# A depthwise convolution's third input tile, prepared one layer earlier: where the transposes, the residual store and the first weights are placed

## The chip, the cores and the metric

The kernel runs on one core of one Trainium2 chip. The metric is the device time of one execution in microseconds. The core has a matrix engine (PE), a vector engine (DVE), a scalar engine (ACT), a general engine (POOL) and a queue engine (SP) that here only issues transfers. Sixteen DMA engines move data between DRAM and the on-chip memory; transfers are issued by SP, by ACT (most weight loads) and by POOL.

## The reference

Input `x` has 8 images of 384 channels of 32x32, all in fp32. Four layers follow, each `x = x + f(groupnorm(x))` with 32 groups:

- layer 0: three depthwise 3x3 convolutions, attention over the 1024 positions with 8 heads, a projection
- layer 1: four experts, each 384 -> 384 -> 384 with ReLU; the two best per position are weighted
- layer 2: a depthwise 7x7 convolution with reflected edges, plus a bias:

```
xp = jnp.pad(x, ((0, 0), (0, 0), (3, 3), (3, 3)), mode='reflect')
out = lax.conv_general_dilated(xp, w, (1, 1), 'VALID', feature_group_count=C) + b
```

- layer 3: three branches of small MLPs and depthwise convolutions (1, 3 and 5), a softmax fusion of them and a projection

The change lies in what layer 1 hands to layer 2, and in layer 2.

## The kernel before

The 384 channels are NC = 3 tiles (`ct`) of P = 128 partitions; B = 8 images of N = 1024 positions. In the profiled execution layer 0 lasts to about 1770 us, layer 1 runs from about 1819 to 2896, layer 2 from 2911 to 3113 and layer 3 from 3123 to the end.

**Layer 1** goes image by image, each in two halves `h` of HF = 512 positions. `experts` loops over 12 pairs of expert and hidden tile. For each, `hidden` does three matmuls (L763) and a ReLU on ACT (L767); DVE multiplies the hidden tile by the expert's coefficient row (L961); three matmuls (L976) add it into three accumulators. The coefficient row `cb` is loaded by `coefs` (L942) from DRAM (`cfmem`) and spread over the partitions, one for each expert and half, from a pool of 5 buffers; the same row times the second bias is added into the residual `r` on DVE (L966). At the end of a half DVE adds the accumulators into `r` (L982). `residual` (L740 to L745) loads and builds the next image's `r`, partly on DVE (L745). In this layer the tile scheduler fixes the order of instructions on each engine from the program; each engine then runs its own order, waiting on semaphores.

When an image is done, `pass_on(r, b)` runs. It stores the finished residual to `r2mem`, for later addition (L1004): for each tile four transfers of 32 partitions, with the channels permuted. It takes the image's group statistics, and for each tile it writes the normalized image `xn2` (affine, ACT L204). Layer 2 wants the image transposed in blocks of 32x32, with three reflected rows at each end (HP = 38 rows instead of H = 32). For tiles 0 and 1 `transpose_in` does that at once into `xts[0]` and `xts[1]`, which stay on the chip: a DVE transpose (L989) and two POOL copies of the edges (L992, L993). For tile 2 there is no third such tile yet: `xn2` is stored as it is to `x2mem` (L1017).

**Layer 2** is written as banded matmuls (L1327): for each tile 16 weight tiles (8 values of `c`, two halves `e`) with 28 matmuls of 256 columns each. A weight tile is made in two steps. `load_weights` loads two of them at once as `w` (L1052, issued by ACT; the first two by SP), and POOL adds the edge columns (L1056). `next_weights` spreads one into `wx` with two ACT instructions (L1068), from a pool of three that opens when layer 1's pools close, and it calls `load_weights` after each second one. From layer 2 on the order of instructions is the written one.

During tile 1 of layer 2, `prepare(b)` (L1163) makes `xts[2]`, in the memory of `xts[0]`, two images after each of four steps: load from `x2mem` (L1168), then `transpose_in`. The output of a tile is evicted by ACT (L1268) and finished during the next tile by `finish` (L1174 to L1206): DVE transposes it back (L1180), SP loads the stored residual (`r2`, L1183), DVE adds it with the bias (L1185), SP stores the sum (`y2mem`, L1188), and DVE takes statistics. `finish_all` runs these steps for the eight images at a pace given by a table of counts, one count for each `c`.

**Transfers.** Each issuing engine handles its transfers in the order written, and waits in front of one until what it needs is there. SP's and ACT's transfers also share eight completion counters, given out in program order: a transfer that gets a counter first waits until the transfer that had it before, most often the one eight places earlier, has landed. If that one was issued by the other engine, the two queues are tied together.

Of the kernel before, what the change touches and what calls it, by code (L numbers as in the profile page):

```python
# [11 lines left out]
FP = mybir.dt.float32  # L12
# [6 lines left out]
P = 128  # L19
B, C, H, W = 8, 384, 32, 32  # L20
N = H * W
NC = C // P
HF = 512
# [32 lines left out]
K7, R7 = 7, 3  # L56
HP = H + 2 * R7
# [13 lines left out]
def img(a):  # L71
    return a.rearrange("p (h w) -> p h w", w=W)
# [3 lines left out]
def conv_mixer_kernel(ctx: ExitStack, tc: tile.TileContext, a: dict, out: bass.AP):  # L76
    nc = tc.nc
# [5 lines left out]
    dram = ctx.enter_context(tc.tile_pool(name="raw", bufs=1, space=DRAM))  # L83
# [42 lines left out]
    with tc.tile_pool(name="gprep", bufs=1) as gp, tc.tile_pool(  # L126
        name="gpsum", bufs=2, space=PSUM
# [115 lines left out]
    with (  # L243
# [9 lines left out]
        with tc.tile_pool(name="cx", bufs=4) as cx, tc.tile_pool(  # L253
            name="cgn", bufs=2, space=PSUM
        ) as cgn:
            for b in range(B):
                x = cx.tile([P, NC - 1, N], FP, tag="x", name="x")
# [457 lines left out]
    pre_pool.close()  # L715


    r2mem = [dram.tile([P, B, N], FP, tag=f"r2_{ct}", name=f"r2_{ct}") for ct in range(NC)]
    x2mem = dram.tile([P, B, N], FP, tag="x2m", name="x2mem")
    y2mem = [dram.tile([NC, P, N], FP, tag=f"y2_{b}", name=f"y2_{b}") for b in range(B)]  # L720
    mv3 = const.tile([P, 2, NC, B], FP, name="mv3")

# [215 lines left out]
    ex = ewpool.enter_context(tc.tile_pool(name="ex", bufs=2, reuse_waits="tile"))  # L938

    def coefs(b, h, e):  # L940
        cb = ex.tile([P, HF], FP, tag="cb", name="cb", bufs=5)
        nc.sync.dma_start(  # L942
            out=cb,
            in_=cfrows[2 * b + h : 2 * b + h + 1, e * HF : (e + 1) * HF].to_broadcast([P, HF]),
        )
        return cb
# [37 lines left out]

    xts = []

    def transpose_in(xt, b, xn):

        nc.vector.transpose(  # L989
            xt[:, :, b, R7 : R7 + H].rearrange("p c h -> p h c"), img(xn)  # L990
        )
        nc.gpsimd.tensor_copy(xt[:, :, b, 0:R7], xt[:, :, b, 2 * R7 : R7 : -1])  # L992
        nc.gpsimd.tensor_copy(  # L993
            xt[:, :, b, R7 + H : HP], xt[:, :, b, R7 + H - 2 : H - 2 : -1]
        )

    def new_xt(pool):
        return pool.tile([P, 32, B, HP], FP, tag="xt", name="xt")

    def pass_on(r, b):  # L1000

        for ct in range(NC):
            for i in range(4):
                nc.sync.dma_start(  # L1004
                    out=r2mem[ct][:, b, :].rearrange("(d b a r) n -> a b d r n", a=2, b=2, d=2)[
                        i // 2, i % 2
                    ],
                    in_=r[32 * i : 32 * i + 32, ct, :],
                )
        s, t = gn_coefs(image_stats(r), eh, "sm")  # L1010
        for ct in range(NC):
            xn2 = ex.tile([P, N], FP, tag="xn2", name="xn2")
            affine(xn2, r[:, ct, :], s[:, ct : ct + 1], t[:, ct : ct + 1])
            if ct < 2:
                transpose_in(xts[ct], b, xn2)
            else:
                nc.sync.dma_start(out=x2mem[:, b, :], in_=xn2)  # L1017

    for b, h in EARLY:
        experts(rs[b].tile, b, h)  # L1020
# [12 lines left out]
    lw = lwpool.enter_context(  # L1033
        tc.tile_pool(name="lw", bufs=2, side="right", reuse_waits="tile")
    )
    parity = lw.tile([P, 2], FP, name="parity", bufs=1)
    nc.gpsimd.memset(parity, 0.0)
    for i in range(4):
        nc.gpsimd.memset(parity[32 * i : 32 * i + 32, i % 2 : i % 2 + 1], 1.0)
    WPARTS = {K7: 2, 5: 2, 3: 1}  # L1040
    weights, loaded = {}, []
    todo_load = [(K7, ct, c) for ct in range(NC) for c in range(8)]
# [18 lines left out]
    def next_weights():  # L1061
        if not loaded:
            return
        key, w = loaded.pop(0)
        n = w.shape[1]
        x = wx.tile([P, 2 * K7, 2, W], FP, tag="wx", name="wx")
        for t in range(2):
            nc.scalar.activation(x[:, :n, t, :], w, AF.Copy, scale=parity[:, t : t + 1])  # L1068
        weights[key] = x.rearrange("p r t w -> p r (t w)")
        if key[3] == WPARTS[key[0]] - 1:  # L1070
            load_weights()
# [5 lines left out]
    for b in range(B):  # L1077
        if b == B - 1:
            for _ in range(2):
                load_weights(nc.sync)  # L1080
        if b < KEPT:
            r = rs[b].tile
        else:
            r = er.tile([P, NC, N], FP, tag="r", name="r")
            for _ in residual(b, [r[:, ct, :] for ct in range(NC)], ex, 2):
                pass
        for h in range(2):
            if (b, h) not in EARLY:
                experts(r, b, h)
        pass_on(r, b)  # L1090
# [1 line left out]
    wpool.close()  # L1092
    early_pool.close()
    wxpool = ExitStack()
    wx = wxpool.enter_context(tc.tile_pool(name="wx", bufs=3, side="right", reuse_waits="tile"))
    for _ in range(3):
        next_weights()


# [60 lines left out]
    hmem = [dram.tile([MR, N], FP, tag=f"h{b}", name=f"h{b}") for b in range(B)]  # L1160
    fmem = dram.tile([P, 3, B + HB], FP, tag="fac", name="fmem")

    def prepare(b):  # L1163

        if b == 0:
            xts.append(new_xt(xa))
        xn2 = ty.tile([P, N], FP, tag="xn2", name="xn2")
        nc.sync.dma_start(out=xn2, in_=x2mem[:, b, :])  # L1168
        transpose_in(xts[2], b, xn2)

    def new_y():
        return ty.tile([P, N], FP, tag="y", name="y", bufs=4)
# [4 lines left out]
    def finish(ct, b, o, y):  # L1177
        if y is None:
            y = new_y()
        nc.vector.transpose(img(y), o[:, b])  # L1180
        yield
        r2 = ty.tile([P, N], FP, tag="r2", name="r2")
        nc.sync.dma_start(out=r2, in_=r2mem[ct][:, b, :])  # L1183
        yield
        nc.vector.scalar_tensor_tensor(  # L1185
            out=y, in0=y, scalar=b7[:, ct : ct + 1], in1=r2, op0=ALU.add, op1=ALU.add
        )
        nc.sync.dma_start(out=y2mem[b][ct], in_=y)  # L1188
        bs = small.tile([P, 2, 6], FP, tag="gn_bs", name="gn_bs")
        bn_stats_of(bs, y)  # L1190
        nc.vector.bn_aggr(mv3[:, :, ct, b], bs.rearrange("p a s -> p (a s)"))
        if ct == 2:
            return
        e = edges[:, ct, b]
        v = img(y).rearrange("p (g r) w -> p g r w", r=2)[:, ::15]
        nc.vector.tensor_reduce(
            sums[:, ct, b, 1:].rearrange("p (g r) -> p g r", r=2), v, AX.X, ALU.add
        )
        v = img(y).rearrange("p h (g r) -> p g r h", r=2)[:, ::15]
        nc.vector.tensor_reduce(e[:, 0].rearrange("p (g r) -> p g r", r=2), v, AX.X, ALU.add)  # L1200
        for g in range(2):
            nc.gpsimd.tensor_copy(
                e[:, 1 + 2 * g : 3 + 2 * g].rearrange("p r (k s) -> p r k s", s=2),
                img(y)[:, 30 * g : 30 * g + 2, :].rearrange("p r (k s) -> p r k s", s=2)[:, :, ::15],
            )
# [109 lines left out]
    with tc.manual_schedule(engines=ORDERED | {mybir.EngineType.Pool}):  # L1315

        for ct in range(NC):
            o = None
            for c in range(8):
                if c % 2 == 0:  # L1320
                    ps = group(B)
                for e in range(2):
                    w = weights.pop((K7, ct, c, e))
                    for k in range(K7):
                        for d, i in product(range(2), repeat=2):
                            r = slice(64 * i, 64 * i + 64)
                            nc.tensor.matmul(  # L1327
                                ps[64 * d : 64 * d + 64, 2 * i + e, c % 2],
                                lhsT=w[r, d * K7 + k, :],
                                rhs=xts[ct][r, 16 * d + 8 * e + c, :, k : k + H],  # L1330
                                start=k == 0, stop=k == K7 - 1,
                            )
                    next_weights()
                if c == 0:
                    if ct > 0:
                        rest = finish_all(ct - 1, last_o)
                        next(rest)
                    o = to.tile([P, B, H, 32], FP, tag="o", name="o")
                if c % 2:
                    evict(o, ps, c - 1)  # L1340
                for _ in range(((0,) * 8, (0, 1, 1, 1, 1, 1, 2, 1), (0, 2, 2, 2, 2, 0, 0, 0))[ct][c]):
                    next(rest, None)
                if ct == 1 and c >= 1 and c < 5:
                    for b in (2 * c - 2, 2 * c - 1):
                        prepare(b)
                if ct == 0 and c == 2:
                    load3()
                if ct == 2 and c == 5:
                    norm01 = gn_steps((mv3[:, 0, :2], mv3[:, 1, :2]), Banks, order="B")
                    next(norm01)  # L1350
                if ct == 2 and c == 6:
                    s01, t01 = next(norm01)
                    for o2, v in ((pair_s, s01), (pair_t, t01)):
                        for half in range(2):
                            nc.vector.tensor_copy(
                                o2[64 * half : 64 * half + 64, :],
                                v[0:64, 1, half * HB : (half + 1) * HB],
                            )
                    for q in range(HB):
                        prepare3(1, q)  # L1360
            last_o = o
# [516 lines left out]
```

## Time and profile before

| | |
|---|---|
| median of 3 runs | 3455.18 us (3448.89 to 3457.11) |
| the profiled execution | 3452.46 us |
| its span in the trace | 3450.7 us |
| mean granted TensorE clock | 0.964 |
| busy PE / DVE / ACT / POOL | 91% / 47% / 38% / 4% |
| transfers at L1004 (residual store) | 96 of 128 KB |
| transfers at L1017 and L1168 (`x2mem`) | 8 of 512 KB each |

The profile's page lists the busy time of each engine, the span in slices, the DMA queues, the chain of work that ended last, and the costliest groups of instructions. A line of the timeline gives start, duration, engine, source line, operation, output and input, how many instructions were merged, and in brackets how long the engine had been idle before and what it waited for. Times count from the start of the span. Stretches of PE inside layer 2, from the table of windows: between 2945 and 2980 PE is busy for 34.90 us of 35; between 3015 and 3050 for 20.30 of 35, at a granted clock of 0.76.

### The profile page before, as it was taken

The numbers are of one execution on the slowest core, as the hardware profiler recorded it, in microseconds if no ns is written. First come the engines' busy times: TensorE is split into PE (matmuls) and PEld (weight loads), VectorE is DVE, ScalarE is ACT, GpSimd is POOL, SyncE is SP. The second block draws the span as 40 slices with busy tenths as digits, with TensorE's granted clock in tenths as the row PEclk, the third lists the DMA queues.
The fourth block names the chain that finished last, engine by engine and source line by source line (L and its number), as shares of the span: only waits on it lengthen the run. The fifth ranks groups of instructions, "written<-read, shape, count | busy, mean of one in ns | idle before, by whom it ended". The sixth has DMA issues, their size and how long they took to land. (4 is left out here: it accounts for less than half of the span.)

```text
span 3450.7 us, 46880 instructions
## 1 busy us (share of the span) xinstructions
PE 3128.2 (91%) x20224; PEld 1427.4 (41%) x20224; DVE 1609.7 (47%) x2193; ACT 1304.5 (38%) x1339; POOL 151.4 (4%) x337
## 2 busy tenths in 40 slices
PE   3666999999999999999979999999999997975989
PEld 2443333343434343434333444444444443655444
DVE  6788344444444535444453643333333331356164
ACT  3654453535354545444425212222121111546530
POOL 1000000000000000000010000000000000111200
PEclk9988999999999999999989999999999998987999
DMA  6766111020111111100027222012021011566666
GB/s 231 246 237 247 74 34 63 21 76 21 60 37 57 40 57 34 56 28 19 23 74 267 70 86 76 23 69 76 21 75 64 15 37 35 197 231 212 228 197 201
DMA packets 96799, 337.89 MB, mean 98 GB/s; under 512 B 13769, under 2 KB 16417, under 8 KB 92137
## 3 DMA queue, kind: packets, MB, share of 16 engines
q1 hardware_dynamic: 73736, 265.37, 21.8%
q10 hardware_dynamic: 13776, 36.90, 3.4%
q0 software_dynamic: 9072, 32.56, 2.7%
q8 instruction: 160, 2.62, 0.3%
q14 instruction: 55, 0.44, 0.0%
HBM read 236.39 MB, written 101.53 MB: 98 GB/s over the span
## 5 line engine op out<-in xcount | busy, mean ns | idle before, releaser
L552 ACT ACTIVATE e<-sc 128x1024 f32<-128x1024 f32 x512 | 484.2, 1029 | 580.9 <-PE sc L545 580.6
L976 PE MATMUL y<-hs,w 128*128 128x512 f32 x1152 | 530.9, 603 | 25.9 <-DVE hs L961 25.9
L763 PE MATMUL ph<-xn,w 128*128 128x512 f32 x1152 | 525.4, 595 | 0.4 <-ACT xn L204 0.4
L545 PE MATMUL sc<-qT,kT 64*128 64x512 f32 x2048 | 480.0, 605 | 22.6 <-DVE qT L471 15.4
L564 PE MATMUL av<-e,vT 128*64 128x512 f32 x2048 | 468.5, 600 | 0.0
L767 ACT ACTIVATE hs<-ph,b 128x512 f32<-128x512 f32 x192 | 131.6, 685 | 626.0 <-PE ph L763 624.3
L976 PEld LDWEIGHTS y<-hs,w 128*128 128x128 f32 x1152 | 220.3, 193 | 307.0 <-issue 263.6
L763 PEld LDWEIGHTS ph<-xn,w 128*128 128x128 f32 x1152 | 217.0, 191 | 269.7 <-issue 260.2
L545 PEld LDWEIGHTS sc<-qT,kT 64*128 64x128 f32 x2048 | 186.2, 186 | 309.6 <-issue 231.7
L961 DVE TENSOR_TENSOR hs<-hs,cb 128x512 f32<-128x512 f32 x192 | 130.5, 689 | 344.8 <-ACT hs L767 338.5
L564 PEld LDWEIGHTS av<-e,vT 128*64 128x64 f32 x2048 | 135.8, 137 | 317.7 <-issue 317.7
L453 PE MATMUL sc<-y,pw 128*128 128x512 f32 x576 | 253.8, 602 | 11.3 <-DVE kT L471 6.6
L329 PE MATMUL ps<-xt,w 32*32 32x256 f32 x6912 | 166.2, 431 | 96.8 <-issue 96.8
L580 DVE RECIPROCAL inv<-sm 128x512 f32<-128x512 f32 x64 | 214.6, 3353 | 2.2
L1327 PE MATMUL ps<-xt,wx 64*64 64x256 f32 x2688 | 162.2, 401 | 41.6 <-ACT wx L1068 41.4
L966 DVE SCALAR_TENSOR_TENSOR r<-cb,b,r 128x512 f32<-128x512 f32 x192 | 134.9, 745 | 136.2 <-DMA cb<-cfmem 134.7
L578 DVE LOAD_MASK_SELECT sm<-av x64 | 0.9, 14 | 417.1 <-PE av L564 417.1
L329 PEld LDWEIGHTS ps<-xt,w 32*32 32x32 f32 x6912 | 113.7, 109 | 149.0 <-issue 125.4
L453 PEld LDWEIGHTS sc<-y,pw 128*128 128x128 f32 x576 | 110.3, 193 | 154.3 <-issue 146.3
L354 ACT COPY o<-ps 128x2048 f32<-128x2048 f32 x36 | 134.4, 3735 | 95.5 <-PE ps L329 92.3
L1068 ACT ACTIVATE wx<-w,parity 128x448 f32<-128x448 f32 (+2 forms) x192 | 108.1, 615 | 125.9 <-DMA r<-r 29.9
L1327 PEld LDWEIGHTS ps<-xt,wx 64*64 64x64 f32 x2688 | 106.2, 141 | 96.5 <-ACT wx L1068 37.0
(290 smaller groups left out, 2768.5 us busy)
## 6 DMA issues: line engine op xcount, KB each, us to landing
raw<-y SPq DMA_DIRECT2D x72, 512.0 KB
y<-raw SPq DMA_DIRECT2D x24, 1536.0 KB
xr<-in_x SPq DMA_DIRECT2D x42, 512.0 KB
cb<-cfmem SPq DMA_DIRECT2D x64, 256.0 KB
w<-in_w ACTq DMA_DIRECT2D x36, 384.0 KB
x<-in_x SPq DMA_DIRECT2D x16, 768.0 KB
z<-z POOLq DMA_DIRECT2D x16, 768.0 KB, 4.2
r<-z SPq DMA_DIRECT2D x24, 512.0 KB
```

Source lines behind the costliest of these rows:

```text
L329: nc.tensor.matmul(ps[32 * j : 32 * j + 32, i, cc], lhsT=w[r, cc, j, k, :], rhs=xt0s[ct][r, 8 * j + 2 * u + cc, :, k : k + H], start=k == ...
L354: nc.scalar.copy(o.rearrange("p b h (i c) -> p i c (b h)", i=4)[:, :, 2 * u : 2 * u + 2], ps.rearrange("p i c b h -> p i c (b h)"),)
L453: nc.tensor.matmul(ps[:, h, :], lhsT=w[:, ct, pair, :], rhs=y[:, ct, h * HF : (h + 1) * HF], start=ct == 0, stop=ct == NC - 1,)
L545: nc.tensor.matmul(sc[:, s, :], lhsT=kTs[b][r, pair, m * P : (m + 1) * P], rhs=qTs[b][r, pair, h * HF : (h + 1) * HF], start=True, stop=True,)
L552: nc.scalar.activation(e, sc, AF.Exp, scale=1.0 if shifted else HD**-0.5)
L564: nc.tensor.matmul(av[64 * s : 64 * s + 64, :], lhsT=vT[:, m, c0 : c0 + 64], rhs=e[:, s, :], start=m == 0, stop=m == N // P - 1,)
L580: nc.vector.reciprocal(inv, sm)
L763: nc.tensor.matmul(ph, lhsT=w1[:, e, ct, dc * P : (dc + 1) * P], rhs=xn[:, ct, :], start=ct == 0, stop=ct == NC - 1,)
L767: nc.scalar.activation(hs, ph, AF.Relu, bias=b1[:, e, dc : dc + 1])
L966: nc.vector.scalar_tensor_tensor(out=out[oc], in0=cb[e], scalar=b2[:, oc, e : e + 1], in1=out[oc], op0=ALU.mult, op1=ALU.add,)
L976: nc.tensor.matmul(py[oc], lhsT=w2[:, e, dc, oc * P : (oc + 1) * P], rhs=hs, start=k == 0, stop=k == len(TODO) - 1,)
L1327: nc.tensor.matmul(ps[64 * d : 64 * d + 64, 2 * i + e, c % 2], lhsT=w[r, d * K7 + k, :], rhs=xts[ct][r, 16 * d + 8 * e + c, :, k : k + H], ...
```

## The change

- `r2mem` is laid out by image instead of by tile, and the residual is stored by four transfers of 32 partitions with all three tiles in one row of 12 KB, instead of twelve with rows of 4 KB.
- The third tile is transposed and its edges are copied in layer 1 too, into a new one-buffer tile `x2`. It is stored into `x2mem`, which has now the layout of `xts[2]` in which the image is the third index: 32 runs of 38 floats (152 bytes) for each partition.
- `prepare(c)` only loads: eight transfers, each of every eighth of the 32 rows for all images (4 rows of 8 x 38 floats a partition) straight into `xts[2]`.
- The pool of `cb` has 4 buffers instead of 5.
- The first `wx` is spread inside layer 1, at the last image, into a pool of its own (`lwx`); the fourth, seventh and so on use that pool again. The `wx` pool has 2 buffers.
- The table of counts for `finish_all` differs in the rows of tiles 1 and 2.

```diff
-    r2mem = [dram.tile([P, B, N], FP, ...) for ct in range(NC)]
-    x2mem = dram.tile([P, B, N], FP, tag="x2m", name="x2mem")
+    r2mem = [dram.tile([P, NC, N], FP, ...) for b in range(B)]
+    x2mem = dram.tile([P, 32, B, HP], FP, tag="x2m", name="x2mem")
...
-        cb = ex.tile([P, HF], FP, tag="cb", name="cb", bufs=5)
+        cb = ex.tile([P, HF], FP, tag="cb", name="cb", bufs=4)
...
-        for ct in range(NC):
-            for i in range(4):
-                nc.sync.dma_start(
-                    out=r2mem[ct][:, b, :].rearrange("(d b a r) n -> a b d r n", a=2, b=2, d=2)[
-                        i // 2, i % 2
-                    ],
-                    in_=r[32 * i : 32 * i + 32, ct, :],
-                )
+        for i in range(4):
+            nc.sync.dma_start(
+                out=r2mem[b].rearrange("(d b a r) c n -> a b d r (c n)", a=2, b=2, d=2)[i // 2, i % 2],
+                in_=r[32 * i : 32 * i + 32].rearrange("p c n -> p (c n)"),
+            )
...
             if ct < 2:
-                transpose_in(xts[ct], b, xn2)
+                transpose_in(xts[ct][:, :, b], xn2)
             else:
-                nc.sync.dma_start(out=x2mem[:, b, :], in_=xn2)
+                x = ex.tile([P, 32, HP], FP, tag="x2", name="x2", bufs=1)
+                transpose_in(x, xn2)
+                nc.sync.dma_start(out=x2mem[:, :, b], in_=x)
...
-        x = wx.tile([P, 2 * K7, 2, W], FP, tag="wx", name="wx")
+        n_spread.append(key)
+        x = wxs[len(n_spread) % 3 != 1].tile([P, 2 * K7, 2, W], FP, tag="wx", name="wx")
...
             for _ in range(2):
                 load_weights(nc.sync)
+            next_weights()
...
-    wx = wxpool.enter_context(tc.tile_pool(name="wx", bufs=3, side="right", ...))
-    for _ in range(3):
+    wxs.append(wxpool.enter_context(tc.tile_pool(name="wx", bufs=2, side="right", ...)))
+    for _ in range(2):
         next_weights()
...
-    def prepare(b):
+    def prepare(c):
...
-        xn2 = ty.tile([P, N], FP, tag="xn2", name="xn2")
-        nc.sync.dma_start(out=xn2, in_=x2mem[:, b, :])
-        transpose_in(xts[2], b, xn2)
+        nc.sync.dma_start(out=xts[2][:, c::8], in_=x2mem[:, c::8])
...
-        nc.sync.dma_start(out=r2, in_=r2mem[ct][:, b, :])
+        nc.sync.dma_start(out=r2, in_=r2mem[b][:, ct, :])
...
-    ... ((0,) * 8, (0, 1, 1, 1, 1, 1, 2, 1), (0, 2, 2, 2, 2, 0, 0, 0))[ct][c]
+    ... ((0,) * 8, (0, 1, 1, 1, 2, 1, 1, 1), (0, 1, 2, 2, 2, 1, 0, 0))[ct][c]
```

In the changed kernel the lines move by a few numbers: the residual store is L1000, the `x2mem` store L1013, the transpose L990, the weight load L1053, the spread L1070, the load of the third tile L1170, the load of the residual L1184.

More of the change, by code (lines that the diff above doesn't have):

```diff
@@ L715, in conv_mixer_kernel @@
     pre_pool.close()
-    r2mem = [dram.tile([P, B, N], FP, tag=f"r2_{ct}", name=f"r2_{ct}") for ct in range(NC)]
-    x2mem = dram.tile([P, B, N], FP, tag="x2m", name="x2mem")
+    r2mem = [dram.tile([P, NC, N], FP, tag=f"r2_{b}", name=f"r2_{b}") for b in range(B)]
+    x2mem = dram.tile([P, 32, B, HP], FP, tag="x2m", name="x2mem")
     y2mem = [dram.tile([NC, P, N], FP, tag=f"y2_{b}", name=f"y2_{b}") for b in range(B)]
@@ L985, in conv_mixer_kernel, with transpose_in @@
     xts = []
-    def transpose_in(xt, b, xn):
-        nc.vector.transpose(
-            xt[:, :, b, R7 : R7 + H].rearrange("p c h -> p h c"), img(xn)
-        )
[L992 to L995, printed above, removed]
+    def transpose_in(x, xn):
+        nc.vector.transpose(x[:, :, R7 : R7 + H].rearrange("p c h -> p h c"), img(xn))
+        nc.gpsimd.tensor_copy(x[:, :, 0:R7], x[:, :, 2 * R7 : R7 : -1])
+        nc.gpsimd.tensor_copy(x[:, :, R7 + H : HP], x[:, :, R7 + H - 2 : H - 2 : -1])
     def new_xt(pool):
@@ L1000, in pass_on @@
     def pass_on(r, b):
-        for ct in range(NC):
-            for i in range(4):
-                nc.sync.dma_start(
-                    out=r2mem[ct][:, b, :].rearrange("(d b a r) n -> a b d r n", a=2, b=2, d=2)[
-                        i // 2, i % 2
-                    ],
-                    in_=r[32 * i : 32 * i + 32, ct, :],
-                )
+        for i in range(4):
[3 more added lines that the diff above has]
+            )
         s, t = gn_coefs(image_stats(r), eh, "sm")
@@ L1035, in conv_mixer_kernel @@
     )
+    lwx = lwpool.enter_context(
+        tc.tile_pool(name="lwx", bufs=1, side="right", reuse_waits="tile")
+    )
     parity = lw.tile([P, 2], FP, name="parity", bufs=1)
@@ L1039, in conv_mixer_kernel @@
         nc.gpsimd.memset(parity[32 * i : 32 * i + 32, i % 2 : i % 2 + 1], 1.0)
+    wxs = [lwx]
+    n_spread = []
     WPARTS = {K7: 2, 5: 2, 3: 1}
@@ L1094, in conv_mixer_kernel @@
     wxpool = ExitStack()
-    wx = wxpool.enter_context(tc.tile_pool(name="wx", bufs=3, side="right", reuse_waits="tile"))
-    for _ in range(3):
+    wxs.append(wxpool.enter_context(tc.tile_pool(name="wx", bufs=2, side="right", reuse_waits="tile")))
+    for _ in range(2):
         next_weights()
@@ L1161, in conv_mixer_kernel @@
     fmem = dram.tile([P, 3, B + HB], FP, tag="fac", name="fmem")
-    def prepare(b):
-        if b == 0:
+    def prepare(c):
+        if c == 0:
             xts.append(new_xt(xa))
-        xn2 = ty.tile([P, N], FP, tag="xn2", name="xn2")
-        nc.sync.dma_start(out=xn2, in_=x2mem[:, b, :])
-        transpose_in(xts[2], b, xn2)
+        nc.sync.dma_start(out=xts[2][:, c::8], in_=x2mem[:, c::8])
     def new_y():
@@ L1340, in conv_mixer_kernel @@
                     evict(o, ps, c - 1)
-                for _ in range(((0,) * 8, (0, 1, 1, 1, 1, 1, 2, 1), (0, 2, 2, 2, 2, 0, 0, 0))[ct][c]):
+                for _ in range(((0,) * 8, (0, 1, 1, 1, 2, 1, 1, 1), (0, 1, 2, 2, 2, 1, 0, 0))[ct][c]):
                     next(rest, None)
                 if ct == 1 and c >= 1 and c < 5:
-                    for b in (2 * c - 2, 2 * c - 1):
-                        prepare(b)
+                    for c2 in (2 * c - 2, 2 * c - 1):
+                        prepare(c2)
                 if ct == 0 and c == 2:
```

## The prediction

> **What bounds the kernel now.** I read the page's busy shares first, then the chain that ended last, then the waits and timeline of the two stages touched. The busy line of PE and the chain's shares by engine and by line:
>
> ```profile
> PE 3128.2 (91%) x20224; PEld 1427.4 (41%) x20224; DVE 1609.7 (47%) x2193; ACT 1304.5 (38%) x1339; POOL 151.4 (4%) x337
> ...
> PE 28%; DMA 9%; DVE 4%; ACT 2%; issue 2%; SPq 1%; POOL 0%; ACTq 0%; DVEq 0%; POOLq 0%
> PE ph L763 11%; PE y L976 10%; DMA cb<-cfmem 3%; DMA r<-r 3%; DMA w<-in_w 1%; PE po L1705 1%; PE po L1708 1%; PE po L1716 1%; SPq L1004 1%; ACT o L1268 1%; PE ps L1327 1%; DMA ya<-y 1%; PE ps L1294 1%; PE ps L1493 1%; DVE gn_bs L144 1%
> ```
>
> PE is the bound at 91%; what a DMA edit can win or lose is PE's idle time, and two transfers stand in the chain for it: cb and the residual r. In layer 1 the timeline shows, for the image ending at 2227 (all engines, lines picked):
>
> ```profile
> 2227.95 17.34 SPq L1004 DMA_DIRECT2D r<-r  x12
> ...
> 2245.39 0.37 SPq L1017 DMA_DIRECT2D x2mem<-xn  x1
> ...
> 2263.07 2.08 DVE L966 SCALAR_TENSOR_TENSOR r<-cb,b,r 128x512 f32<-128x512 f32 x3 [8.30 <-DMA cb<-cfmem]
> 2265.06 2.48 DVE L745 SCALAR_TENSOR_TENSOR r<-r,zn_s,xr 128x1024 f32<-128x1024 f32 x2
> ...
> 2268.20 5.38 PE L976 MATMUL y<-hs,w 128*128 128x512 f32 x6 [4.59 <-DVE hs L961]
> ```
>
> The reader is to see a queue: twelve residual stores, the x2mem store, then the cb load (issued at 2246.30, landed 16.75 us later by the chain), all on SP's rings; DVE stands in order at L966 for that cb, and the L961 that PE needs is behind it. So PE loses 4.59 us. The same gap stands after the other images: 1.84, 4.50, 4.59, 3.87, 4.16, 4.33, 1.52, together 24.8 us. In layer 2, PE's and ACT's timelines:
>
> ```profile
> 2930.65 82.82 PE L1327 MATMUL ps<-xt,wx 64*64 64x256 f32 x1456 [11.54 <-ACT wx L1068]
> 3029.63 39.75 PE L1327 MATMUL ps<-xt,wx 64*64 64x256 f32 x672 [16.16 <-ACT wx L1068]
> 3074.74 14.53 PE L1327 MATMUL ps<-xt,wx 64*64 64x256 f32 x224 [5.36 <-ACT wx L1068]
> ```
> ```profile
> 2929.93 1.79 ACT L1068 ACTIVATE wx<-w,parity 128x448 f32<-128x448 f32 x3 [17.74 <-DMA k<-in_k]
> 3028.35 2.35 ACT L1068 ACTIVATE wx<-w,parity 128x448 f32<-128x448 f32 x4 [21.09 <-DMA r<-r]
> ```
>
> ACT's spread needs neither k nor r. SP's and ACT's loads share eight completion counters in program order, so ACT's L1052 waits until the DMA eight places earlier has landed, and its spreads queue behind it. At 2930 that DMA lies behind the last image's residual store; at 3028 it is an r2 load (issued 3023.64) of a finish chain that DVE runs from 2981.6 to 3036.8.
>
> **What the Trainium skill says.** "DMA: Bandwidth & Descriptors", "Why a DMA increments its semaphore by 16 and not by 1": the number of engines is the largest divisor up to 16 of the slowest dimension. So a 2x16 store runs on 2 engines. The trace agrees: 2895 to 2911 has a DMA share of 0.12, two in sixteen. The new store's 4096 runs go to 16 engines, 256 each. Its "HWDGE ordering": each engine consumes a ring in order; agreed by the cb wait above. Its "Specifications": under 512 B an engine does read-modify-write; "Why small descriptors are slow" adds a fixed overhead per packet. No store of 152-B runs is in the trace, and this is the unknown, called T: what the new store adds at the tail of engines 0 and 1, which alone carry the residual.
>
> **T, bounded.** Below: the trace's DMA records give one packet 12 ns at 72 B and 16 ns at 200 B; at 152 B an estimate of 14.5 ns, x 256 = 3.7 us. Feed: a 128-run load of 24 B (at 309 us) takes 345 ns from first to last start though each packet takes 9 ns, so 2.7 ns a run over all engines. If that is the supply, 4096 runs take 11.0 us. Part is supplied ahead: 12 issues end after 17.34 us, when about 100 of 192 packets of 159 ns have gone, so a ring holds some 92. Then 256 - 92 = 164 a ring remain when the residual is out: 164 x 16 x 2.7 ns = 7.1 us. Read-modify-write at double the 27 ns of a 512-B packet: 256 x 54 = 13.8 us. I take 7; ends 3.7 and 13.8.
>
> **Part by part.**
>
> Residual, four transfers: 64 packets of 12,288 B per engine, which take 460 ns in layer 0's y<-raw records, 29.4 us, against 192 x 159 ns = 30.5: -1.1. The engine count stays 2. The first of them waits for all three L982 instead of one: +2.5 (a cautious two L982 of 0.69, an L966 of 0.75, and PE's steps between).
>
> x2 store: replaces 8 packets of 159 ns (-1.3) and adds T. In layer 1 it adds a DVE transpose of 1.95 us and two POOL copies of 0.3; the L961 behind it at 2245.10 moves by about that, and PE wants it at 2248.0: hidden with some 0.3 us to spare; without that cover 2 us an image. On SP the store waits for POOL's edge copies, and the cb loads queue behind it; the copies end near 2248, while the residual keeps its engines until about 2259: hidden.
>
> cb with 4 buffers: the load behind the stores is now needed by the first L966 of the next half, one load earlier in the row than with 5. In program order one L966 stands before the L961 that PE wants, where three and two L745 stood: 5.1 us from landing to matmul becomes 1.5, -3.6. But the next cb load waits until that L961 has freed its buffer, and its L966s stand ahead of the next L961: +1 an image (0 to 2).
>
> Per image: -1.1 + 2.5 - 1.3 - 3.6 + T + 1 = T - 2.5. Seven images at T = 7: 7 x 4.5 = +31.5; the first and last gaps (1.84 and 1.52) have less in them than the 3.6 and so less to save, but they do grow. I take +29.
>
> Start of layer 2: one wx is spread in layer 1. That ACT step waits for w and POOL's L1056, done at 2038.19, and the affine behind it was due at 2043.64: hidden; if not, it delays one image by some us. Two more remain, so PE starts about 1.6 us earlier (2909 instead of 2910.6). This wins nothing: the next L1052 now waits on the counter of the last x2 store, behind the residual, and PE stands before the third wx as now. Landing: first store +1.5 (three L982 with nothing between), -1.1, and k1 and x2mem's 2 us replaced by T: +5.4 at T = 7.
>
> Second tile: 8 DVE transposes (15.6 us) and 16 POOL copies leave the finish chain. Its last r2 loads move some 15 us earlier, with ACT's lanes hanging on them. Walking the lanes in order leaves about 3 us (0 to 6) of the 16.16: -13. After the idle stretch PE's windows show clock 0.76 at 3015 to 3050 against 1.00 at 2980 to 3015, and a wx takes 4.25 us instead of 3.09: some 4 us less: -17 together (-11 to -21). The 8 L1170 loads (5 MB, 12.5 us of all engines by 159 ns per 4 KB) stand together on SP, gated by PE leaving the first tile; y2 stores and r2 loads queue behind them, 12.5 us that DVE's eight transposes (9.2 us) mostly cover. The r2 loads read the same 4 KB rows from the new place: 0. The 5.36 before the last tile's third quarter has the same lane pattern: 0. The order of the small layer-3 loads and the finish pacing: 0, within the same slack.
>
> Sum at T = 7: +29 + 5.4 - 17 = +17.4. Against the profiled run's own 3452.46 (span 3450.7) that is 3470; the median of the runs, 3455.18, is 2.7 above that run, so **3472**.
>
> **Rivals.**
> - A, faster: T near 3.7. Per image +1.2 gives 7 x 1.2 = +8, start +2, second tile -17 to -21: -7 to -11, and without the extra +1 per image down to -18: 3437 to 3448. For it: 13-ns packet durations, and the 512-B store of 128 runs at 1937 keeps engines over 90% busy. Against it: the 24-B load leaves them under half busy. It decides below T = 4.7, where the sum is about -5 and falling.
> - B, much slower: read-modify-write, T = 13.8. 7 x 11.3 = +79, start +12, second tile -15: +76, 3531. With T = 10: +52 + 8 - 15 = +45, 3500. For it: the skill's row. Against it: no small-store train here shows such durations.
> - C, the second tile's stall stays: the loads standing together delay the first r2 loads and ACT's w loads, and the wait of 16 becomes 10. Then +17.4 + 8 = 3480 at T = 7.
> - D, the moved work changes nothing: T near 5, gain and loss cancel, 3450 to 3462.
>
> **How the numbers follow.** T about 7 (5.5 to 9): 0.37; A 0.32; D 0.13; B with T above 9: 0.13; C 0.05. About 0.3%, 10 us, is what a measurement tells from no change; A counts as faster, D as same, the rest 0.55 as slower. Range 8 in 10: from the middle of A, 3440, to 3512, T about 11. The likeliest case alone: 3460 to 3490.
>
> **What would show it.** The seven layer-1 gaps before L976 at about 8 to 10 us, with DVE L966 waiting on cb; their size minus about 2 is T. If they stay at or below 4.6, A holds. PE's gap before the third wx ending near 2935 plus what layer 1 shifted. In the second tile, ACT L1068's wait of 21 us gone and PE's gap 16.16 down to 6 or less; if it is above 10, the lane walk is wrong. Residual packets should take about 460 ns on two engines. The prediction is wrong if the residual no longer runs on two engines, if L961 after the third transpose becomes late, or if the DVE order around L966 isn't what sets PE's wait.

## The result

The changed kernel is slower: 3491.99 us (median of 4 runs, 3483.90 to 3498.14) against 3456.14 (4 runs, 3448.89 to 3460.56). The ratio is 1.0104, 95% interval 1.0075 to 1.0134. The forecast was 3472, with a range of 3440 to 3512 and slower as the likeliest sign. The sign and the range hold. The size was about half of what came: forecast +17.4 on the profiled execution, measured +35.7 on its span (3486.4 against 3450.7).

First the page of the changed kernel: busy shares and the chain by engine and by line.

```profile
PE 3131.7 (90%) x20224; PEld 1428.6 (41%) x20224; DVE 1608.2 (46%) x2193; ACT 1304.4 (37%) x1339; POOL 146.0 (4%) x337
...
PE 32%; DMA 8%; DVE 3%; ACT 1%; issue 1%; SPq 1%; POOL 0%; ACTq 0%; DVEq 0%; POOLq 0%
```

PE has nearly the same work (3131.7 us busy against 3128.2); almost all of the new time is PE standing still. The list of PE's waits from the first image's end in layer 1 to the start of layer 3 says for what (engine, line, what it waited for, us in total, times, longest). First before, then after:

```profile
PE ps L1327 <- ACT wx L1068: 41.4, 5, 16.2
PE y L976 <- DVE hs L961: 25.9, 10, 4.6
```
```profile
PE y L976 <- DVE hs L961: 62.7, 7, 12.2
PE ps L1328 <- ACT wx L1070: 28.5, 6, 13.1
PE ps L1328 <- POOL xt L991: 5.1, 1, 5.1
```

Layer 1's gaps went from 24.8 us (the 25.9 hold three waits that are too short to count as gaps) to 62.7. Layer 2's waits for weights went from 41.4 to 28.5. The timeline of one image of layer 1 after the change, all engines, lines picked:

```profile
2101.31 4.06 SPq L1000 DMA_DIRECT2D r<-r  x4
...
2118.56 0.57 SPq L1013 DMA_DIRECT2D x2mem<-x  x1
2119.22 20.85 SPq L942 DMA_DIRECT2D cb<-cfmem  x1
2140.30 0.80 SPq L742 DMA_DIRECT2D r<-z  x2
2145.19 0.75 DVE L966 SCALAR_TENSOR_TENSOR r<-cb,b,r 128x512 f32<-128x512 f32 x1 [19.62 <-DMA cb<-cfmem]
...
2146.60 3.78 PE L976 MATMUL y<-hs,w 128*128 128x512 f32 x4 [12.17 <-DVE hs L961]
```

SP gets rid of the residual in 4.06 us of issuing instead of 17.34 and then meets the new store. Behind it the issue of one cb load takes 20.85 us. In the kernel with long runs, below, it takes 1.86, so the short runs in front of it hold it; that the queues of engines 0 and 1 are full is how I read this, and no view shows it. DVE gets its cb 43.9 us after the first residual store (2145.19 - 2101.31), where it was 35.1 in the image that the prediction shows and 34.5 to 34.6 in the others. From there to the matmul it is 1.4 us, where it was 5.1 in that image.

Where the 35.7 us are, by PE's starts in the two traces:

| stretch | before | after | difference |
|---|---|---|---|
| start to PE's first matmul of layer 2 | 2910.61 | 2949.20 | +38.6 |
| from there to the end of the wait before the third weight tile | 20.04 | 26.33 | +6.3 |
| from there to layer 3's first matmul | 192.75 | 180.86 | -11.9 |
| layer 3 | 327.3 | 330.0 | +2.7 |

The first row is 37.9 us of longer gaps, -2.1 for the wait at the head of layer 2 (7.20 to 5.08) and 2.8 before and between.

### The profile page after: what moved, and what is told of

Its sections match the earlier page's. It is cut to its first block, busy times and chain, and to the rows that moved or that the text cites. A ratio compares the mean times of both kernels' runs of the same rounds, so it can differ in the third digit from the quotient of the medians.

```text
span 3486.4 us, 46805 instructions
## 1 busy us (share of the span) xinstructions
PE 3131.7 (90%) x20224; PEld 1428.6 (41%) x20224; DVE 1608.2 (46%) x2193; ACT 1304.4 (37%) x1339; POOL 146.0 (4%) x337
## 5 line engine op out<-in xcount | busy, mean ns | idle before, releaser
L976 PE MATMUL y<-hs,w 128*128 128x512 f32 x1152 | 533.8, 606 | 62.7 <-DVE hs L961 62.7
L961 DVE TENSOR_TENSOR hs<-hs,cb 128x512 f32<-128x512 f32 x192 | 130.0, 687 | 324.3 <-ACT hs L767 318.6
L966 DVE SCALAR_TENSOR_TENSOR r<-cb,b,r 128x512 f32<-128x512 f32 x192 | 135.0, 746 | 190.8 <-DMA cb<-cfmem 189.0
L1328 PE MATMUL ps<-xt,wx 64*64 64x256 f32 x2688 | 163.4, 403 | 33.9 <-ACT wx L1070 28.5
L1070 ACT ACTIVATE wx<-w,parity 128x448 f32<-128x448 f32 (+2 forms) x192 | 108.4, 614 | 216.6 <-POOL w L1057 108.4
```

The source lines that it names most:

```text
L966: nc.vector.scalar_tensor_tensor(out=out[oc], in0=cb[e], scalar=b2[:, oc, e : e + 1], in1=out[oc], op0=ALU.mult, op1=ALU.add,)
L976: nc.tensor.matmul(py[oc], lhsT=w2[:, e, dc, oc * P : (oc + 1) * P], rhs=hs, start=k == 0, stop=k == len(TODO) - 1,)
L1328: nc.tensor.matmul(ps[64 * d : 64 * d + 64, 2 * i + e, c % 2], lhsT=w[r, d * K7 + k, :], rhs=xts[ct][r, 16 * d + 8 * e + c, :, k : k + H], ...
```

## The experiments

The seven gaps after the change were not alike: 3.3, 12.2, 11.2, 7.2, 7.4, 11.0 and 10.4 us. My theory explains this by the places of the runs: image b's runs begin at 152 b bytes. If DRAM is counted in pieces of 32 B, those at a run's ends are written in part: one a run for images 0, 3, 4 and 7 (the quick places), two for 1, 2, 5 and 6 (the slow ones). A piece that a run covers only in part is called part-written here. Rivals: the number of runs alone; the residual's later start; the four buffers of cb; the residual's new rows.

**The images' places swapped in pairs** (`SLOT` is 1, 0, 3, 2, 5, 4, 7, 6).

```diff
-                nc.sync.dma_start(out=x2mem[:, :, b], in_=x)
+                nc.sync.dma_start(out=x2mem[:, :, SLOT[b]], in_=x)
...
-        nc.vector.transpose(img(y), o[:, b])
+        nc.vector.transpose(img(y), o[:, SLOT[b] if ct == 2 else b])
```

> The changed kernel with the images' places in x2mem swapped in pairs (0 with 1, 2 with 3, 4 with 5, 6 with 7); nothing else moves. My theory: image b's runs of 152 B begin at 152 b, so they leave one 32-B piece of DRAM half written for b = 0, 3, 4, 7 and two for b = 1, 2, 5, 6, and half-written pieces are what slows the store and the residual beside it. Then the layer-1 gaps follow the place, not the image: images 1, 2, 5, 6 fall from 12.2, 11.2, 11.0, 10.4 to about 7.3 us, images 3 and 4 rise from 7.2 and 7.4 to about 11 and image 0 from 3.3 to about 7; sum about 60 as now. Rival: the pattern belongs to the images (what runs beside them), or the number of runs alone sets the cost: then the gaps stay as they are, 12, 11, 7, 7, 11, 10.

PE's timeline for images 1 to 3, first with the places swapped, then the changed kernel:

```profile
2151.23 5.28 PE L976 MATMUL y<-hs,w 128*128 128x512 f32 x6 [7.37 <-DVE hs L961]
2289.17 4.58 PE L976 MATMUL y<-hs,w 128*128 128x512 f32 x6 [7.76 <-DVE hs L961]
2429.97 5.49 PE L976 MATMUL y<-hs,w 128*128 128x512 f32 x6 [11.25 <-DVE hs L961]
```
```profile
2146.60 5.49 PE L976 MATMUL y<-hs,w 128*128 128x512 f32 x6 [12.17 <-DVE hs L961]
2288.14 4.81 PE L976 MATMUL y<-hs,w 128*128 128x512 f32 x6 [11.23 <-DVE hs L961]
2424.79 4.75 PE L976 MATMUL y<-hs,w 128*128 128x512 f32 x6 [7.20 <-DVE hs L961]
```

The pattern turned over: all seven gaps are 11.1, 7.4, 7.8, 11.3, 11.3, 8.1 and 6.1 us. In layer 1 only addresses in DRAM moved. So it is the destination address that decides between 7 and 11, not the image, the source or the count. The miss: image 0 went to 11.1, not 7. This kernel and the two that follow ran once each; what is read is the gaps of that one trace, whose six or seven images repeat each other.

**Runs padded to 160 B, and runs of 176 B at a pitch of 192.** These write padding too, which POOL sets to zero, and load the third tile by 152-B runs; only their layer 1 is read. The diff is that of the first; the second has 48 and 44 in place of the two 40, and stores into the first 44 of the 48.

```diff
-    x2mem = dram.tile([P, 32, B, HP], FP, ...)
+    x2mem = dram.tile([P, 32, B, 40], FP, ...)
...
-                x = ex.tile([P, 32, HP], FP, tag="x2", name="x2", bufs=1)
+                x = ex.tile([P, 32, 40], FP, tag="x2", name="x2", bufs=1)
```

> The changed kernel with runs padded to 160 B in x2mem (40 floats, all stored), so that every 32-B piece is written whole; the count of runs stays 4096. Read only layer 1 of it: layer 2 loads the third tile by 152-B runs here, some 30 us of every engine instead of 12, and may be longer. My theory (half-written pieces): the small packets fall to about 14 ns throughout, the residual takes about 30 us, and the seven gaps become alike at 5 to 6 us (the first about 2), sum about 35 instead of 62.7. Rival (the number of runs sets it): gaps stay between 7 and 12, sum about 60.

> The changed kernel with runs of 44 floats (176 B, the last 6 are padding) at a pitch of 192 B: each run starts on a 32-B boundary, writes five pieces of 32 B whole and half of a sixth. So far two things go together: runs that touch six pieces (five in the quick images and in the 160-B runs), and runs with two pieces written in part (one or none there). Read only layer 1: the load of the third tile is by 152-B runs here. If the number of touched pieces sets the cost, all images but the first have gaps of about 10 to 12 us and cb lands 42 to 44 us after the first residual store. If the second part-written piece sets it, all have gaps of about 7 and cb lands at about 39.

The same three images, 160 B first, 176 B second:

```profile
2143.30 5.49 PE L976 MATMUL y<-hs,w 128*128 128x512 f32 x6 [7.40 <-DVE hs L961]
2280.39 5.48 PE L976 MATMUL y<-hs,w 128*128 128x512 f32 x6 [6.67 <-DVE hs L961]
2417.68 5.10 PE L976 MATMUL y<-hs,w 128*128 128x512 f32 x6 [7.17 <-DVE hs L961]
```
```profile
2148.90 5.49 PE L976 MATMUL y<-hs,w 128*128 128x512 f32 x6 [8.35 <-DVE hs L961]
2287.59 4.75 PE L976 MATMUL y<-hs,w 128*128 128x512 f32 x6 [7.88 <-DVE hs L961]
2425.10 4.27 PE L976 MATMUL y<-hs,w 128*128 128x512 f32 x6 [7.97 <-DVE hs L961]
```

Both are even, as forecast, with sums of 42.9 and 50.1 instead of 62.7. The 176-B runs touch six pieces, as the slow places do, but only one in part, and they are quick: so it is the second part-written piece that costs about 4 us an image. But whole pieces brought only 7, not the 5 to 6 that I expected: with nothing written in part there are still 4096 short runs, and they cost most of what they cost in the quick places. The size of 32 B is singled out by the places alone, if the buffer starts on such a boundary: in pieces of 16 B every image's runs would have one end in part, and in pieces of 64 B images 3 and 4, which were quick, would have two.

**The third tile image by image.** The memory of the third tile is viewed as image, row, position; the matmuls read the same values at other strides, and store and loads have runs of 4864 B.

```diff
-    x2mem = dram.tile([P, 32, B, HP], FP, ...)
+    x2mem = dram.tile([P, B, 32, HP], FP, ...)
...
-                nc.sync.dma_start(out=x2mem[:, :, b], in_=x)
+                nc.sync.dma_start(out=x2mem[:, b], in_=x)
...
-            xts.append(new_xt(xa))
+            x = new_xt(xa).rearrange("p c b h -> p (c b h)")
+            xts.append(x.rearrange("p (b c h) -> p c b h", b=B, c=32))
-        nc.sync.dma_start(out=xts[2][:, c::8], in_=x2mem[:, c::8])
+        nc.sync.dma_start(out=xts[2][:, :, c], in_=x2mem[:, c])
```

> The changed kernel with x2mem and the third tile laid out image by image, so that the store writes 128 runs of 4864 B and the loads read the same; the matmuls read the same values at other strides. My theory: the store costs 8 packets of about 190 ns an engine, 1.5 us, and slows nothing; by the prediction's formula, T - 2.5 with T = 1.5, the gaps become about 1 us smaller than before the change (sum about 18), the start of layer 2 falls by 4 us: about 3445 us, ratio to before 0.997, 47 us below the changed kernel. Rival (the later start of the residual, the four buffers of cb or the third transpose cost the time, not the short runs): no more than 10 us below the changed kernel, gaps of 8 and more.

Measured 3454.00 us, ratio to before 0.9995 (0.9987 to 1.0004): 38 us below the changed kernel, and level with before. The table of windows of the changed kernel and of this one, image 1 (window and its length, then each engine's busy time, PE's clock, DMA share of 16 engines, GB/s):

```profile
2105.00:2119.00 14.00, 14.00 (x49) 7.54 (x48) 7.95 (x12) 4.87 (x5) 2.63 (x7) 1.00 0.13 54
2119.00:2121.00 2.00, 2.00 (x6) 0.81 (x6) 0.69 (x1) 0.69 (x1) 0.00 (x0) 1.00 0.64 150
2121.00:2129.00 8.00, 8.00 (x20) 3.57 (x19) 0.69 (x1) 0.69 (x1) 0.00 (x0) 1.00 1.24 70
```
```profile
2105.00:2119.00 14.00, 14.00 (x48) 7.36 (x47) 8.15 (x12) 4.87 (x5) 2.62 (x7) 1.00 0.13 55
2119.00:2121.00 2.00, 2.00 (x6) 0.95 (x5) 0.69 (x1) 0.69 (x1) 0.00 (x0) 1.00 0.76 297
2121.00:2129.00 8.00, 8.00 (x20) 3.52 (x19) 0.69 (x1) 0.69 (x1) 0.00 (x0) 1.00 0.25 87
```

Until 2119 both are the residual alone on two engines: a share of 0.13. Then the 4864-B runs are gone within about 3 us, but for the share of engines 0 and 1. The short runs fill all engines for 8 more us (a share over 1: packets overlap), and all engines together move 70 GB/s. The trace's DMA records say what happens in it: packets of 152 B take 13 to 14 ns in the first 2 us and about 50 to 60 ns after, and the residual's 12,288-B packets on engines 0 and 1 rise from 460 ns to about 1050 and stay there until the short runs of the other engines are out. The residual's last packet ends 35.4 us after its first starts in image 1, and 30.5 us with the 4864-B runs. At the quick places (images 3 and 4 of the changed kernel) the same records are mild: the short packets take about 20 ns for 2 us and 14 again after that, the residual's packets are at about 750 ns for those 2 us only, and the residual takes 31.3 and 31.5 us.

The sum of gaps fell to 29.5, not to 18. DVE's timeline shows why:

```profile
2135.73 2.08 DVE L966 SCALAR_TENSOR_TENSOR r<-cb,b,r 128x512 f32<-128x512 f32 x3 [9.94 <-DMA cb<-cfmem]
2138.92 0.68 DVE L961 TENSOR_TENSOR hs<-hs,cb 128x512 f32<-128x512 f32 x1
```

cb came 34.2 us after the first store, but the scheduler has put three L966 and an L745 in front of the L961 again: 3.9 us to the matmul at 2139.66 instead of 1.4. So the 38 us hold a loss of about 2.5 us an image by the order, and the long runs alone are worth more than that.

**The residual alone in four transfers; four buffers of cb alone; the spread alone.** Each is the kernel before with one part of the change: the r2mem layout with L1000 and L1184; `bufs=5` to `bufs=4` on the cb tile; the `lwx` pool and the call in layer 1.

```diff
-    r2mem = [dram.tile([P, B, N], FP, ...) for ct in range(NC)]
+    r2mem = [dram.tile([P, NC, N], FP, ...) for b in range(B)]
...
-        cb = ex.tile([P, HF], FP, tag="cb", name="cb", bufs=5)
+        cb = ex.tile([P, HF], FP, tag="cb", name="cb", bufs=4)
...
+            next_weights()
```

> The kernel before with only the residual stored by four transfers of 12-KB rows. By the prediction's terms -1.1 + 2.5 = +1.4 us an image, seven images and the start of layer 2: about +10 us, ratio 1.003, gaps of 3 to 6 us. Rival: the few large rows free SP early enough for the cb load to be issued sooner, and the gaps shrink: ratio 0.995 to 1.000. If this alone made the kernel 1% slower, the short runs would not be the cause.

> The kernel before with 4 buffers of cb instead of 5, nothing else. The prediction priced this at -3.6 + 1 us an image where the order on DVE leaves one L966 ahead of the L961 that PE wants. If that order comes from the four buffers, the seven gaps fall from 24.8 to about 8 to 10 and the ratio is 0.995 to 0.997. If the order is the scheduler's answer to the whole change, the buffers alone give at best nothing (ratio 0.999 to 1.001), and at worst one cb load less in hand makes the gaps longer (ratio 1.001 to 1.004).

> The kernel before with only the weights' part of the change: the first wx spread inside layer 1 into a pool of its own, two more after. The prediction priced it at nothing, since PE stands before the third wx either way: ratio 0.999 to 1.001. Rival: the ACT step that waits for w and for POOL holds back the affine behind it at the end of image 0, or the other counters that the loads get make new waits in layer 2: ratio 1.001 to 1.004, a gap that the kernel before has not, near 2045 or in layer 2.

Measured, in this order: 1.0019 (1.0011 to 1.0027), 0.9992 (0.9977 to 1.0006), 0.9994 (0.9986 to 1.0001). The four transfers cost about 6.5 us (0.0019 x 3456) where +10 was expected; the gaps are 28.6 instead of 24.8. They are less than expected because one L745 moved behind the L961 in this kernel: about 4.0 us from cb to the matmul where it was about 5.2. Neither of the others can be told from nothing, though the gaps with four buffers sum to 20.5. None alone has the one-L966 order: in image 1 of all three DVE runs three L966 after cb and then L745, as here with the four buffers alone:

```profile
2129.72 2.08 DVE L966 SCALAR_TENSOR_TENSOR r<-cb,b,r 128x512 f32<-128x512 f32 x3 [7.94 <-DMA cb<-cfmem]
2131.72 2.48 DVE L745 SCALAR_TENSOR_TENSOR r<-r,zn_s,xr 128x1024 f32<-128x1024 f32 x2
```

**The changed kernel with the residual in twelve transfers again.** `r2mem` is laid out by tile again, and so is its load.

```diff
-        for i in range(4):
-            nc.sync.dma_start(out=r2mem[b].rearrange(...)[i // 2, i % 2], in_=r[32 * i : 32 * i + 32].rearrange("p c n -> p (c n)"))
+        for ct in range(NC):
+            for i in range(4):
+                nc.sync.dma_start(out=r2mem[ct][:, b, :].rearrange(...)[i // 2, i % 2], in_=r[32 * i : 32 * i + 32, ct, :])
```

> The changed kernel with the residual stored as before, by tile in twelve transfers with rows of 4 KB; the 152-B runs, the 4 buffers of cb and the early spread stay. My theory: the short runs still slow the residual beside them and stand behind it, so the gaps stay at 6 to 12 us, sum 50 to 65, two heights by place as in the changed kernel: 3480 to 3492, ratio 1.007 to 1.0105; the four transfers are worth no more than the 6 us that they cost alone. Rival (the 12-KB rows make the residual suffer under the short runs, where 4-KB rows would take turns): the gaps fall to 4 to 6 us, 3465 or less, ratio below 1.003.

Measured 1.0148 (1.0118 to 1.0178), slower than either expectation; the gaps sum to 73.4.

```profile
2145.29 2.08 DVE L966 SCALAR_TENSOR_TENSOR r<-cb,b,r 128x512 f32<-128x512 f32 x3 [19.07 <-DMA cb<-cfmem]
2149.22 3.78 PE L976 MATMUL y<-hs,w 128*128 128x512 f32 x4 [14.14 <-DVE hs L961]
```

The short runs act as before (4-KB packets beside them rise from 159 to about 500 ns), so the rival with the rows is out. What is lost is the short order: three L966 again. In image 1 cb lands 10.2 us after PE's gap opens, where it was 10.8 in the changed kernel, but the matmul follows after 3.9 us instead of 1.4. Beside the short runs the four transfers are thus worth something, though alone they cost: by way of the scheduler's order, not of the DMA.

**The residual over 16 engines.** Eight transfers of 16 partitions, so that the slowest dimension is 16. Put into the kernel before (with the layout of `r2mem` by image and its load), the changed kernel, and the image-by-image one.

```diff
-        for i in range(4):
+        for i in range(8):
             nc.sync.dma_start(
-                out=r2mem[b].rearrange("(d b a r) c n -> a b d r (c n)", a=2, b=2, d=2)[i // 2, i % 2],
-                in_=r[32 * i : 32 * i + 32].rearrange("p c n -> p (c n)"),
+                out=r2mem[b].rearrange("(d b a r) c n -> a b d r (c n)", a=2, b=2, d=2)[i // 4, i // 2 % 2, i % 2],
+                in_=r[16 * i : 16 * i + 16].rearrange("p c n -> p (c n)"),
             )
```

> The kernel before with the residual stored by image in eight transfers over 16 engines. The seven gaps (24.8 us) go, and the wait of 11.5 us before the third weight tile shrinks to 0 to 3; the 16 us wait in the second tile stays: about 33 us less, 3420 to 3430, ratio 0.990 to 0.992. Against r16_after it tells what the rest of the change is worth once the residual is out of the way: my theory says 5 to 10 us for the change, all of it in the second tile.

> The changed kernel with the residual stored by eight transfers of 16 partitions, whose slowest dimension is 16, so that 16 engines carry it instead of 2: 8 packets of 460 ns an engine, 3.7 us instead of 29.4. My theory (what costs the time is the queue on the two engines that hold the residual, with the short runs behind and beside it): the cb load lands 15 us early, the seven gaps (62.7 us) go, and the 13 us wait at the start of layer 2 falls to 0 to 4: about 70 us below the changed kernel, 3415 to 3425, ratio 0.988 to 0.991. Rival (the short runs are slow in themselves, wherever the residual goes): the x2 store of 4 to 11 us still delays cb and gaps of 3 to 8 us stay: 3450 to 3470.

> Both: the third tile stored in runs of 4864 B and the residual over 16 engines. 29.5 us of gaps and some 9 of the wait at the start of layer 2 go from the image-major kernel's 3454: 3410 to 3420, ratio 0.987 to 0.990; the same as r16_after within 5 us if short runs cost only beside and behind the residual, 10 us or more below it if they cost by themselves.

| kernel | us | ratio to before (95%) |
|---|---|---|
| before + 16 engines | 3414.64 | 0.9884 (0.9864 to 0.9904) |
| changed + 16 engines | 3404.65 | 0.9862 (0.9839 to 0.9885) |
| image by image + 16 engines | 3409.74 | 0.9875 (0.9857 to 0.9894) |

PE's waits in the changed kernel with 16 engines:

```profile
PE ps L1328 <- ACT wx L1070: 17.7, 6, 5.3
...
PE y L976 <- DVE hs L961: 5.0, 2, 3.8
```

The gaps are gone but for the first, and in the kernel before with 16 engines none is over 0.8 us:

```profile
PE y L976 <- DVE hs L961: 5.1, 8, 0.8
```

The first two are some 5 to 10 us better than I expected, the third is at the edge. The whole change now wins 10 us against the same residual store without it, as expected, though the two intervals overlap; the wait for weights in layer 2 is 17.7 us here and 29.0 in the kernel before with 16 engines:

```profile
PE ps L1324 <- ACT wx L1065: 29.0, 3, 16.7
```

The records show the cost of the short runs on its own here, with the residual out 9 us earlier: from first to last packet 9.8 us in image 1 and 5.3 in image 3, where the 4864-B store of image 0, also clear of its residual, took 2.2. After the first image it costs nothing in layer 1, because PE does not wait for what stands behind it. The image-by-image version is not better, which the theory allows. The changed kernel with the residual over 16 engines beats both kernels of this case: 50 us below before, 87 below the changed one.

## Why the prediction was right, and where its size was off

- **Queue on engines 0 and 1 with cb behind it: right.** Taking the residual off the two engines removed both kernels' gaps. What the Trainium skill says of the count of engines ("DMA: Bandwidth & Descriptors", "Why a DMA increments its semaphore by 16 and not by 1") held in both directions: slowest dimension 2, DMA share 0.13; slowest dimension 16, the same bytes in 8.6 us instead of 30.4.
- **The residual's later start (+2.5): right.** PE's gap opens 33.1 us after the first store (2134.43 - 2101.31) where it was 35.7. **Its own term (-1.1): right in sign, too large.** Packets take 460 ns where nothing is beside them, 30.4 us for 64, but with the four transfers alone cb landed only 0.5 us sooner after the first store (34.1 for 34.65, the average of images 1 to 6).
- **The third transpose, hidden: right.** PE's seven gaps of layer 1 are its only waits for the L961.
- **One L966 ahead of the L961: right for this kernel (-3.6 forecast, -3.4 on average), but by luck.** The prediction had it from the four buffers of cb, and with these alone it did not come; no single part had it. The **+1 for the next cb load** didn't show: gaps and landings agree without it. Image 2's cb landed 42.9 us after the first store, 7.8 later than before; +2.5 for the start and -3.7 for the order (1.4 for 5.1) make 6.6, and its gap grew by 11.23 - 4.59 = 6.64.
- **T: the term that was mis-sized.** With the four transfers alone cb landed 34.1 us after the first store; less the 1.3 of that kernel's own x2mem store, it would land after 32.8 without any. In the changed kernel it landed after 43.9, 42.9, 38.9, 39.2, 42.7 and 42.1 (images 1 to 6), so T is 8.8 us on average, 6.2 at the quick places and 10.1 at the slow, where I took 7. With it -0.5 + 2.5 - 1.3 - 3.4 + 8.8 makes 6.1 us an image, which is by how much these six gaps grew on average.

  T is also not what the prediction said it was, a tail of runs on engines 0 and 1 held up by their feed. That tail is 3.8 to 4.3 us, close to the lower bound of 3.7; clear of the residual a whole store at a quick place took 5.3 us, 1.3 ns a run, so a feed of 2.7 ns a run isn't what sets it. The rest is what the prediction lacks, in two parts. The short runs of the other 14 engines, which it took as free, slow the residual on the first two: from 30.5 us to 31.3 and 31.5 at the quick places, and to 33.9 to 35.4 at the slow. And the held issue keeps the cb load off all engines, not only off those two. In image 1 cb's first packet starts 39.4 us after the first store and its last ends at 43.5; in the image-by-image kernel 112 of its 128 packets have started by 22.1, and only the last 16 wait for the residual. So from the last short run to cb it takes 1.7 to 3.4 us, where it takes 1.0 in that kernel.
- **The Trainium skill's "under 512 B" row** ("DMA: Bandwidth & Descriptors", "Specifications") was priced as double a 512-B packet, 54 ns, for every run, 13.8 us: too much by far for the tail, though the short packets beside the residual took about that at the slow places. What the runs show that fits a read-modify-write is the cost of part-written pieces: about 4 us an image for the second one. That a DRAM read stands behind it was not seen; only the dependence on the destination address was.
- **Start of layer 2: right.** Forecast +5.4, measured +4.2 (-2.1 before PE's first matmul, +6.3 from there); ACT's spread waits as said:

```profile
2974.81 0.67 ACT L1070 ACTIVATE wx<-w,parity 128x448 f32<-128x448 f32 x1 [16.88 <-DMA x2mem<-x]
```

- **Second tile: the mechanism right, the size too large.** The 16.16 us wait became 4.15, 2.08 and 1.33, together 7.6 where 3 was forecast and 10 was its rival C. Forecast was -17 with 4 us of regained clock; the whole rest of layer 2 gave -11.9, of which PE's gaps are 10.0. So about 2 us are left for the clock, which no run isolates. Two waits remain, on transfers of SP's finish chain:

```profile
3049.20 2.35 ACT L1070 ACTIVATE wx<-w,parity 128x448 f32<-128x448 f32 x4 [8.26 <-DMA y<-x]
3059.00 1.23 ACT L1070 ACTIVATE wx<-w,parity 128x448 f32<-128x448 f32 x2 [7.46 <-DMA r<-r]
```

  Ahead of them SP spends 10.12 us on issuing the eight L1170 loads together (3021.80), before the first y2 store (3037.00). That these loads cause the remainder is argued from the order, not shown by a run.
- **What no term covers:** 2.8 us before and between in the first two layers, and 2.7 in layer 3. Single executions differ by as much; no run explains them.

Together: layer 1's gaps +37.9 for +29, layer 2 -7.7 for -11.6, and 5.5 of other things.

## What to carry to other kernels

Price a store of short runs at what it does to the other transfers in flight, not only at its own packets' time: here it slowed a neighbour's packets up to about twofold, and what stood behind both paid. Look first at how many engines a transfer uses: a store whose slowest dimension was 2 ran on 2 of 16, and splitting it by its rows was worth more than anything in the change. Where a scheduler orders an engine, look at its order in each variant before giving an edit credit for it.

## What the runs showed of the hardware

- A store of 4096 runs of 152 B, clear of other stores, took 4.9 to 6.3 or 9.8 to 11.6 us for 622 KB, by its address alone: with one or two part-written pieces of 32 B a run. Runs of 160 B and of 176 B behaved much like the quick case.
- Beside it at a slow place, another store's 12,288-B packets on two of the engines took about 850 to 1100 ns instead of 460, and 4-KB packets about 350 to 500 instead of 159; at a quick place 12,288-B packets took about 750, for 2 us.
- Behind the short runs and the residual the issue of one cb load was held for 16.6 to 20.9 us; behind 4864-B runs and the same residual it took 1.8.
- Spreading 1.5 MB over 16 engines took 8.6 us from first to last packet instead of 30.4 on two; its packets took about 800 to 930 ns instead of 460, so the gain was 3.5 times, not eight.
